# A four-layer macaron network on one Trainium2 core: expert rows, moments and norms by chunk, and another order in the mixers' fronts

## The chip, the cores and the metric

The kernel runs on one core of one Trainium2 chip. The metric is the device time in microseconds (us) of one execution; the time given for a kernel is the median of its runs. The engines are named as in the profile: PE is TensorE (PEld its weight loads), DVE is VectorE, ACT is ScalarE, POOL is GpSimd, SP is SyncE, which here issues most of the DMAs.

## The reference

The input is a stream x of 1024 tokens of 256 features, which goes through four layers. Each layer is a "macaron": half of a feed-forward network, a mixer, and half of a feed-forward network again, each behind a layer norm without weights:

```
def layernorm(x):  m, v = mean(x), var(x);  return (x - m) / sqrt(v + 1e-5)

for layer in 0..3:
    x = x + 0.5 * ffn[layer](layernorm(x))
    x = x +       attn[layer](layernorm(x))
    x = x + 0.5 * ffn[layer](layernorm(x))
```

What the eight blocks compute:

- `ffn[0]`: 32 experts, each token goes to its best 6, weighted by their softmax shares, plus a shared expert. `ffn[3]`: 8 experts, best 2, with a sigmoid router, plus a shared expert. Each expert is `(silu(x Wg) * (x Wu)) Wd`.
- `ffn[1]`: one 256 x 256 linear layer with binarized weights (sign times the mean absolute weight of the row) and a bias. `ffn[2]`: 8 experts of one linear layer, best 1.
- `attn[0]`: retention with 16 heads, a gate, a norm and a multi-layer perceptron. `attn[1]`: sparse attention. `attn[2]` and `attn[3]`: Mamba2 mixers with 8 and 64 heads. They project x, B, C, a gate z and a step dt; run a causal convolution of 4 taps and a silu over x, B and C; turn dt (softplus) and A into decays, with cumulative sums along the chunk; and combine chunk products with a running state.

## The kernel before

**Where the data is.** The stream x stays in SBUF from end to end, as `self.x` of 128 partitions x 8 chunks x 256 features; a chunk is 128 tokens, and 4 chunks (`CB`) are a half b (0 or 1). One method of a class `Net` is a stage; the twelve stages run one after the other in the order of the reference.

**Expert rows and how they reach x.** The expert stages `l0_ffn` and `l3_ffn` (both through `moe`) scatter their results, one row per token and choice (6 or 2 of them), into a table `rows` in HBM, and leave behind, in `self.pending[b]`, a function `add_rows(b)` (L640 to L654). Whoever needs half b of x next calls `settle(b)` (L153), which runs it. `add_rows` takes the half in two pairs of chunks: two DMAs of 768 KB for 6 rows (L644, on SyncE) into a buffer of the five-buffer weight pool, then for each chunk one VectorE add of three rows to three (L648, 128x768) and three adds into x (L651, 128x256). With 2 rows there are two adds. Four places settle: layer 0's mixer, layer 1's first FFN, layer 3's mixer, and the store at the end. The other norms have no rows to add.

**The norm.** `moments(b)` (L171) settles, then does `bn_stats` and `bn_aggr` for each of the 4 chunks on VectorE (L178, L179). `scales(b)` (L182) makes 1/sqrt(v + eps) for the four together on GpSimd, by an add (L187) and a pow (L188) of 128x4. `layernorm` (L191) norms each chunk on VectorE (L193). `transpose_tokens` (L165) turns the four chunks with TensorE (L168), and `evac` copies the PSUM bank of 128x512 to SBUF, by turns on VectorE (L126) and ACT (L128). `layernorm_T` (L202) ties these up as `measure`, `norm`, `turn`, and `row`, which is all three.

**Layer 0's mixer** (`l0_attn`, L707). It has its own `scales(b)` (L734 to L743), which needs two scales per token, hence two pows of 128x4 (L740, L742) per half. Ahead of its loop it runs `scales(0)`, `norm(0)`, `scales(1)`, then issues the loads of fc1 and fc2 on SyncE. The loop of 12 steps is a software pipeline over the chunks: in step s, scores of chunk s-2 (mask add L848), the norm of s+1 (L762 on VectorE, h0 L765 on ACT, two transposes L770), projections of s (L780, L783), rotation of s-1 (`turn`: L793 on GpSimd, L794 and L796 on VectorE), values and gate of s-2, output of s-3 (bias add on GpSimd at L928). Instructions go to each engine's in-order queue in the order of the source.

**Layer 1's FFN** (`l1_ffn`, L1030). For each half: `row(b)` for the whole half, one VectorE add of half the bias to the half (L1038, 128x1024), and for each chunk two matmuls into PSUM (L1042) and a VectorE add into x (L1045). `self.hb` and `self.bwT` (the bias and the transposed weights, both halved) are made ahead of time.

**The mixers of layers 2 and 3** (`mamba`, L1466). Ahead of a loop over steps stands a front, whose order is written out by hand under `in_order`, which keeps TensorE's, ACT's and VectorE's queues in source order (L1835 to L1905). Its pieces: `decay_sums(b)` is a generator in 8 parts, `d0` for half 0 and `d1` for half 1: dt's matmuls (L1518), softplus by Exp and Ln on ACT, dA (L1534), row sums (`ps_row`, L1544), their copy to `cr` and two DMAs into HBM (`rows`), sums `ps_cum` (L1562), and the decays `ps_dec` (L1567). `conv_b`, `conv_c` and `prep_front` each do a projection (L1577), a first tap on ACT (L1580), and give back the other three taps (VectorE, L1584) and a silu (ACT, L1588). `products` multiplies B and C, `prep_back` transposes x (L1659), `chunk` reads decay rows back from HBM, `exponents` (L1687) and `raised` (L1692, an Exp on ACT) turn them into weights. `few` is true for layer 2 (8 heads), where half 1's norm and decay parts lie in the front too; for layer 3 (64 heads) they are put in `later`, part by part, one per step of the loop.

## Time and profile before

| | us |
|---|---|
| runs | 2039.61, 2051.31, 2053.77; median 2051.31 |
| the profiled execution | 2134.34 |
| its span (first to last instruction) | 2132.1, mean granted TensorE clock 0.901 |
| busy in the span: PE, PEld, DVE | 1772.7 (83%), 1258.1 (59%), 1144.8 (54%) |
| busy in the span: ACT, POOL | 798.5 (37%), 879.1 (41%) |
| stretch from layer 0's first rows at 292.84 to its fourth mask add | 55.0 |
| first `l1_ffn`, first rows 744.98 to last add 784.51 | 39.5 |
| second `l1_ffn`, 905.34 to 924.70 | 19.4 |
| front of layer 2's mixer, 1014.0 to 1068.9 | 54.9 |
| front of layer 3's mixer, 1360.77 to 1420.02 | 59.3 |

How to read the profile: times are those of one profiled execution, which took longer than the timed runs. A group of instructions is a line of the code on one engine with its tiles; behind the bar stand its busy time, the mean of one in nanoseconds, and the time that the engine was idle just before them, with what ended that. The table by stretch gives for each engine the busy time and, in brackets, the number of instructions; then the clock that was granted to TensorE as a share of full speed, the busy share of the DMA engines, and GB/s. In the table of waits each line says which instruction waited for which, for how long in all, how many times, and the longest. The timeline gives start, length, engine, line, and in square brackets the idle time ahead. One TensorE matmul in 4-byte floats shows as two records.

### The profile page before, as it was taken

What the parts mean: (1) busy time and instruction counts of PE and PEld (TensorE: products, weight loads), DVE (VectorE), ACT (ScalarE), POOL (GpSimd) and SP (SyncE); (2) the same over time, 40 slices, a digit from 0 to 9 for tenths busy, and PEclk for the clock granted to TensorE, in tenths of its full rate; (3) what the DMA queues carried; (4) which work ended last, traced back from release to release, by engine and by line L of the source; (5) the groups of instructions that cost most, each with busy time, mean ns of one, the idle gap of its engine ahead of it and who ended that gap; (6) DMA issues with size and microseconds to landing.
All of it is one profiled execution on the core that took longest, in us unless ns stands there. A gap on an engine that the chain in (4) does not pass through costs nothing. (4 is left out here: it accounts for less than half of the span.)

```text
span 2132.1 us, 29472 instructions
## 1 busy us (share of the span) xinstructions
PE 1772.7 (83%) x10590; PEld 1258.1 (59%) x10590; DVE 1144.8 (54%) x2679; ACT 798.5 (37%) x1329; POOL 879.1 (41%) x821
## 2 busy tenths in 40 slices
PE   6898849898888737879687988569999999999885
PEld 4576626565666524554366456447777677777564
DVE  5432256316322268656564653377777767776533
ACT  1122214311122204510562012267877677777111
POOL 3466545330666430000042016124566537667253
PEclk8999969998999858979697989789999999999788
DMA  8255450040455340000221013243444444544132
GB/s 286 78 163 157 138 207 12 1 149 24 137 163 159 115 173 1 1 21 0 90 91 31 10 30 96 95 133 119 154 148 149 159 137 154 165 142 128 41 92 91
DMA packets 117438, 226.00 MB, mean 106 GB/s; under 512 B 22382, under 2 KB 68828, under 8 KB 117142
## 3 DMA queue, kind: packets, MB, share of 16 engines
q1 hardware_dynamic: 88134, 170.17, 24.6%
q0 software_dynamic: 20608, 48.45, 7.0%
q10 hardware_dynamic: 8528, 5.26, 0.8%
q8 instruction: 92, 1.51, 0.3%
q14 instruction: 76, 0.62, 0.1%
HBM read 195.13 MB, written 41.81 MB: 111 GB/s over the span
## 5 line engine op out<-in xcount | busy, mean ns | idle before, releaser
L475 POOL DMA_INDIRECT xe<-table,sl_get x176 | 179.8, 1022 | 228.5 <-DVE sl_get L451 146.7
L499 PE MATMUL ps_gu<-we,xeT 128*128 128x352 f32 x704 | 238.1, 481 | 0.0
L529 POOL DMA_INDIRECT rows<-ye,sl_put x176 | 177.0, 1005 | 139.7 <-ACT ye L128 45.6
L524 PE MATMUL ps_ye<-we,hT 88*128 88x256 f32 x704 | 178.6, 396 | 40.7 <-issue 14.1
L1584 DVE SCALAR_TENSOR_TENSOR xc<-pp,L_attn_cols,xc 128x511 f32<-128x511 f32 (+2 forms) x216 | 161.4, 747 | 48.5 <-ACT xc L1580 43.2
L524 PEld LDWEIGHTS ps_ye<-we,hT 88*128 88x128 f32 x704 | 134.7, 195 | 86.7 <-issue 19.6
L504 DVE SCALAR_TENSOR_TENSOR he<-se,xe,ps_gu 128x176 f32<-128x176 f32 x176 | 68.4, 396 | 208.4 <-issue 106.7
L499 PEld LDWEIGHTS ps_gu<-we,xeT 128*128 128x128 f32 x704 | 133.8, 202 | 59.3 <-issue 10.3
L187 POOL TENSOR_SCALAR ln_rstd<-ln_mv 128x4 f32<-128x4 f32 x22 | 5.1, 234 | 393.9 <-DVE ln_mv L179 389.4
L1711 PE MATMUL pz<-xT,wt 128*128 128x128 f32 x1152 | 145.1, 280 | 19.5 <-DVE state L1758 8.0
L1687 DVE SCALAR_TENSOR_TENSOR lm<-lm,jb,top 128x128 f32<-128x128 f32 x576 | 153.6, 340 | 0.0
L1711 PEld LDWEIGHTS pz<-xT,wt 128*128 128x128 f32 x1152 | 137.7, 195 | 25.2 <-issue 9.3
L1577 PE MATMUL pp<-xT,wx 128*128 128x512 f32 x288 | 145.2, 629 | 1.5 <-ACT dec L1568 0.9
L1784 PE MATMUL yacc<-wt,y 128*128 128x256 f32 x576 | 144.1, 393 | 0.7 <-POOL y L1766 0.7
L1766 POOL TENSOR_TENSOR y<-y,sg 128x512 f32<-128x512 f32 x72 | 91.7, 1274 | 108.4 <-DVE y L1765 107.1
L1704 POOL TENSOR_TENSOR ce<-ce,CT 128x1024 f32<-128x1024 f32 x54 | 128.0, 2370 | 0.0
L128 ACT COPY xT<-ps_tr 128x512 f32<-128x512 f32 x22 | 12.8, 584 | 293.4 <-PE ps_tr L168 264.9
L503 ACT ACTIVATE se<-ps_gu 128x176 f32<-128x176 f32 x176 | 54.7, 318 | 172.9 <-PE ps_gu L499 75.8
L1784 PEld LDWEIGHTS yacc<-wt,y 128*128 128x128 f32 x576 | 104.6, 191 | 24.1 <-issue 10.6
L1416 PE MATMUL ps_y<-w8T,xT 128*128 128x512 f32 x256 | 118.5, 617 | 0.0
L1739 PE MATMUL py<-lm,xt 128*64 128x128 f32 x1152 | 109.2, 284 | 6.2 <-issue 5.4
L168 PE MATMUL ps_tr<-cst,xn 128*128 128x128 f32 x176 | 41.9, 394 | 86.5 <-DVE xn L193 67.0
(383 smaller groups left out, 3552.4 us busy)
## 6 DMA issues: line engine op xcount, KB each, us to landing
lm<-rows SPq DMA_DIRECT2D x72, 512.0 KB
ce<-rows SPq DMA_DIRECT2D x54, 512.0 KB
rows<-zero POOLq DMA_DIRECT2D x16, 768.0 KB
y<-rows SPq DMA_DIRECT2D x16, 768.0 KB
we<-in_L_ffn_w_gate_dram SPq DMA_DIRECT2D x64, 176.0 KB
we<-in_L_ffn_w_up_dram SPq DMA_DIRECT2D x64, 176.0 KB
we<-in_L_ffn_w_down_dram SPq DMA_DIRECT2D x64, 176.0 KB
we<-in_L_ffn_w_dram SPq DMA_DIRECT2D x48, 176.0 KB
```

Of the source, the lines that this page charges most:

```text
L475: nc.gpsimd.indirect_dma_start(xe[:, i, :], None, table, bass.IndirectOffsetOnAxis(get[:, e * per + j : e * per + j + 1], 0), bounds_check ...
L499: nc.tensor.matmul(pg, xeT[:, k, i * P : (i + 1) * P], wgu[:, :, k], start=(k == 0), stop=(k == KD - 1))
L524: nc.tensor.matmul(py[:, i, :], hT[:, q, i * P : (i + 1) * P], wd[:, q, :], start=(q == 0), stop=(q == 1))
L529: put_rows = nc.gpsimd.indirect_dma_start(rows, bass.IndirectOffsetOnAxis(put[:, e * per + j : e * per + j + 1], 0), y[:, i, :], None, bou ...
L1416: nc.tensor.matmul(ps, xT[:, k, cs], self.w8T[:, k, 2 * e2 : 2 * e2 + 2, :], start=(k == 0), stop=(k == KD - 1))
L1577: nc.tensor.matmul(pp, wv[:, k, :], xT[:, k, b * S : (b + 1) * S], start=(k == 0), stop=(k == KD - 1))
L1584: nc.vector.scalar_tensor_tensor(out[:, 3 - w :], pp[:, : S - 3 + w], cw[:, m, w : w + 1], out[:, 3 - w :], ALU.mult, ALU.add)
L1687: nc.vector.scalar_tensor_tensor(k["lm"][:, h, :], k["lm"][:, h, :], jb[:, k["c"], n : n + 1], top, ALU.add, ALU.min)
L1704: nc.gpsimd.tensor_tensor(k["ce"], k["ce"], ct, ALU.mult)
L1711: nc.tensor.matmul(pz[:, m, :], u["wz"][:, kk, m * P : (m + 1) * P], xT[:, kk, c * P : (c + 1) * P], start=(kk == 0), stop=(kk == KD - 1),)
L1739: nc.tensor.matmul(py[i * HP : (i + 1) * HP, m, :], w[:, h * HP : (h + 1) * HP], v[:, h, :], start=(m == 0 and n == 0), stop=(n == len(src ...
L1784: nc.tensor.matmul(yacc[cc // 2][:, cc % 2, :], k["y"][:, m, :], u["wo"][:, m, :], start=(u["g"] == 0 and m == 0 and cc % 2 == 0), stop=(u ...
```

## The change

- `self.pending[b]` becomes a list of four functions, one per chunk; `settle(b, n, psum)` runs those of the first n chunks. The rows are still loaded in pairs of chunks by the same DMAs, all of a half at its first chunk.
- New helpers `moment`, `scale` and `centre` do the moments, the 1/sqrt (a pow of one column) and the norm of one chunk.
- Where `psum` is given, the six rows of a chunk are summed by six TensorE matmuls with the identity into a PSUM tile `ps_add`, and one VectorE add puts that into x.
- `l0_attn`: `scales` is by chunk, with one pow of two columns; chunks 0 and 1 go ahead of the loop, and chunk s+2 goes into step s, behind the scores and ahead of the norm of s+1. The loads of fc1 and fc2 are now issued ahead of the second half's rows.
- `l1_ffn` is written anew as a pipeline over 8 chunks in three parts: `front` (rows, moments, scale), `turn` (norm, two transposes, a copy on ACT, the bias add on GpSimd) and `back` (two matmuls, the add into x). Odd chunks' rows, where there are any, are summed on TensorE.
- `layernorm_T`'s `row` goes chunk by chunk (`by_chunks`) where rows are pending: that is half 0 of layer 3's mixer.
- The mixers' front: the projection of x's first block goes ahead of B's taps, the third and fourth decay parts of half 0 ahead of C's taps, and the taps of x's second block behind all eight parts; x's third silu goes ahead of `raised`; for layer 2 the first two parts of `d1` lie together ahead of `raised`; for layer 3 half 1's later parts begin with a free step.
- The store settles chunk by chunk.

The diff, without blank lines:

```diff
...
-    def settle(self, b):
-        if b in self.pending:
-            self.pending.pop(b)()
+    def settle(self, b, n=CB, psum=None):
+        parts = self.pending.get(b, [])
+        while len(parts) > CB - n:
+            parts.pop(0)(psum)
+        if not parts:
+            self.pending.pop(b, None)
...
+    def moment(self, pool, c):
+        st = pool.tile([P, 6], F32, name=f"ln_st{c}")
+        mv = pool.tile([P, 2], F32, name=f"ln_mv{c}")
+        self.nc.vector.bn_stats(st, self.x[:, c, :])
+        self.nc.vector.bn_aggr(mv, st)
+        return mv
+    def scale(self, pool, c):
+        nc = self.nc
+        mv = self.moment(pool, c)
+        rstd = pool.tile([P, 1], F32, name=f"ln_rs{c}")
+        nc.gpsimd.tensor_scalar(rstd, mv[:, 1:2], EPS, None, ALU.add)
+        nc.gpsimd.tensor_tensor(rstd, rstd, self.mhalf[:, 0:1], ALU.pow)
+        return mv, rstd
+    def centre(self, xn, c, mv, rstd):
+        self.nc.vector.tensor_scalar(xn, self.x[:, c, :], mv[:, 0:1], rstd, ALU.subtract, ALU.mult)
+        return xn
     def moments(self, pool, b):
...
         def row(b):
+            if b in self.pending:
+                by_chunks(b)
+                return
             measure(b)
...
+        def by_chunks(b):
+            xn = p.tile([P, CB, D], F32, tag="xn", name="xn")
+            ps = [psum.tile([P, S], F32, tag="mm", name="ps_tr") for _ in range(KD)]
+            ms = {}
+            for cc in range(CB + 1):
+                if cc < CB:
+                    self.settle(b, cc + 1)
+                    ms[cc] = self.scale(p, b * CB + cc)
+                if cc > 0:
+                    j = cc - 1
+                    self.centre(xn[:, j, :], b * CB + j, *ms[j])
+                    for k in range(KD):
+                        self.nc.tensor.transpose(
+                            ps[k][:, j * P : (j + 1) * P], xn[:, j, k * P : (k + 1) * P], self.ident
+                        )
+            for k in range(KD):
+                self.evac(xT[:, k, b * S : (b + 1) * S], ps[k])
         return xT, row, measure, norm, turn
...
-        def add_rows(b):
-            for c0 in range(b * CB, (b + 1) * CB, 2):
-                y2 = self.w("y2")[:, : 2 * K * D].rearrange("p (c n d) -> p c n d", c=2, n=K)
-                for i in range(2):
-                    nc.sync.dma_start(y2[:, i], rv[c0 + i, :, :K, :])
-                for i in range(2):
-                    y, xc, n = y2[:, i], self.x[:, c0 + i, :], K
-                    if n == 6:
-                        nc.vector.tensor_tensor(y[:, 0:3], y[:, 0:3], y[:, 3:6], ALU.add)
-                        n = 3
-                    for j in range(n):
-                        nc.vector.tensor_tensor(xc, xc, y[:, j], ALU.add)
+        ys = {}
+        def add_rows(b, cc, psum):
+            c, pair = b * CB + cc, cc // 2
+            if cc == 0:
+                for q in range(CB // 2):
+                    y2 = self.w("y2")[:, : 2 * K * D].rearrange("p (c n d) -> p c n d", c=2, n=K)
+                    for i in range(2):
+                        nc.sync.dma_start(y2[:, i], rv[b * CB + 2 * q + i, :, :K, :])
+                    ys[b, q] = y2
+            y, xc, n = ys[b, pair][:, cc % 2], self.x[:, c, :], K
+            if psum:
+                ps = psum.tile([P, D], F32, tag="mm", name="ps_add")
+                for j in range(n):
+                    nc.tensor.matmul(ps, self.ident, y[:, j], start=(j == 0), stop=(j == n - 1))
+                nc.vector.tensor_tensor(xc, xc, ps, ALU.add)
+                return
+            if n == 6:
+                nc.vector.tensor_tensor(y[:, 0:3], y[:, 0:3], y[:, 3:6], ALU.add)
+                n = 3
+            for j in range(n):
+                nc.vector.tensor_tensor(xc, xc, y[:, j], ALU.add)
         for b in range(B):
-            self.pending[b] = partial(add_rows, b)
+            self.pending[b] = [partial(add_rows, b, cc) for cc in range(CB)]
...
             h0 = sb.tile([P, NC, D], F32, name="h0")
-            rstd = sb.tile([P, NC], F32, name="ln_rstd")
-            rr = sb.tile([P, NC], F32, name="ln_rr")
+            sc = sb.tile([P, NC, 2], F32, name="ln_sc")
             nb = sb.tile([P, NC], F32, name="ln_nb")
...
-            def scales(b):
-                bs = slice(b * CB, (b + 1) * CB)
-                mv = mvs[b] = self.moments(sb, b)
-                var = mv[:, :, 1]
-                nc.gpsimd.tensor_scalar(rr[:, bs], var, 1.0 + EPS, EPS * EPS, ALU.mult, ALU.add)
-                nc.gpsimd.tensor_tensor(rr[:, bs], rr[:, bs], half[:, :CB], ALU.pow)
-                nc.gpsimd.tensor_scalar(rstd[:, bs], var, EPS, None, ALU.add)
-                nc.gpsimd.tensor_tensor(rstd[:, bs], rstd[:, bs], half[:, :CB], ALU.pow)
-                nc.vector.scalar_tensor_tensor(nb[:, bs], mv[:, :, 0], -1.0, rstd[:, bs], ALU.mult, ALU.mult)
+            def scales(c):
+                self.settle(c // CB, c % CB + 1)
+                mv = mvs[c] = self.moment(sb, c)
+                var = mv[:, 1:2]
+                nc.gpsimd.tensor_scalar(sc[:, c, 0:1], var, 1.0 + EPS, EPS * EPS, ALU.mult, ALU.add)
+                nc.gpsimd.tensor_scalar(sc[:, c, 1:2], var, EPS, None, ALU.add)
+                nc.gpsimd.tensor_tensor(sc[:, c, :], sc[:, c, :], half[:, :2], ALU.pow)
+                nc.vector.scalar_tensor_tensor(
+                    nb[:, c : c + 1], mv[:, 0:1], -1.0, sc[:, c, 1:2], ALU.mult, ALU.mult
+                )
...
                 nc.vector.tensor_scalar(
-                    hn, self.x[:, c, :], mvs[c // CB][:, c % CB, 0:1], rr[:, c : c + 1], ALU.subtract, ALU.mult
+                    hn, self.x[:, c, :], mvs[c][:, 0:1], sc[:, c, 0:1], ALU.subtract, ALU.mult
                 )
                 nc.scalar.activation(
-                    h0[:, c, :], self.x[:, c, :], AF.Identity, bias=nb[:, c : c + 1], scale=rstd[:, c : c + 1]
+                    h0[:, c, :], self.x[:, c, :], AF.Identity, bias=nb[:, c : c + 1], scale=sc[:, c, 1:2]
                 )
...
-            scales(0)
+            for c in range(2):
+                scales(c)
             norm(0)
-            scales(1)
             w2 = self.w("fc1")[:, : KD * F].rearrange("p (k f) -> p k f", k=KD)
...
                     scores(s - 2)
+                if s + 2 < NC:
+                    scales(s + 2)
                 if s + 1 < NC:
...
     def l1_ffn(self):
         nc, tc = self.nc, self.tc
-        with ExitStack() as es:
-            psM = es.enter_context(tc.tile_pool(name="f1m", bufs=8, space=PSUM))
-            xT, row, measure, norm, turn = self.layernorm_T(es, psM)
-            for b in range(B):
-                row(b)
-                xb = self.x[:, b * CB : (b + 1) * CB, :]
-                nc.vector.tensor_tensor(xb, xb, self.hb.unsqueeze(1).to_broadcast([P, CB, D]), ALU.add)
-                for c in range(b * CB, (b + 1) * CB):
-                    ps = psM.tile([P, D], F32, tag="mm", name="ps_y")
-                    for k in range(KD):
-                        nc.tensor.matmul(
-                            ps, xT[:, k, c * P : (c + 1) * P], self.bwT[:, k, :], start=(k == 0), stop=(k == KD - 1)
-                        )
-                    nc.vector.tensor_tensor(self.x[:, c, :], self.x[:, c, :], ps, ALU.add)
+        with tc.tile_pool(name="f1", bufs=3) as sb, tc.tile_pool(name="f1s", bufs=1) as st, tc.tile_pool(
+            name="f1m", bufs=8, space=PSUM
+        ) as psM:
+            ms, xts = {}, {}
+            def front(c):
+                self.settle(c // CB, c % CB + 1, psM if c % 2 else None)
+                ms[c] = self.scale(st, c)
+            def turn(c):
+                xn = self.centre(sb.tile([P, D], F32, tag="xn", name="xn"), c, *ms.pop(c))
+                pt = psM.tile([P, KD, P], F32, tag="mm", name="pt")
+                for k in range(KD):
+                    nc.tensor.transpose(pt[:, k, :], xn[:, k * P : (k + 1) * P], self.ident)
+                xts[c] = sb.tile([P, KD, P], F32, tag="xT", name="xT")
+                nc.scalar.copy(xts[c], pt)
+                nc.gpsimd.tensor_tensor(self.x[:, c, :], self.x[:, c, :], self.hb, ALU.add)
+            def back(c):
+                xT = xts.pop(c)
+                ps = psM.tile([P, D], F32, tag="mm", name="ps_y")
+                for k in range(KD):
+                    nc.tensor.matmul(ps, xT[:, k, :], self.bwT[:, k, :], start=(k == 0), stop=(k == KD - 1))
+                nc.vector.tensor_tensor(self.x[:, c, :], self.x[:, c, :], ps, ALU.add)
+            for c in range(NC + 2):
+                if c < NC:
+                    front(c)
+                if 0 <= c - 1 < NC:
+                    turn(c - 1)
+                if c >= 2:
+                    back(c - 2)
...
                 c_taps, c_silu = conv_c(0)
-                if few:
-                    measure(1)
-                b_taps()
                 next(d0)
...
                 if few:
+                    measure(1)
+                b_taps()
+                next(d0)
+                next(d0)
+                if few:
                     norm(1)
...
                 x[0][0]()
-                next(d0)
                 if few:
...
                     self.settle(1)
-                next(d0)
                 x.append(prep_front(us[0], 1))
-                x[1][0]()
                 next(d0)
...
                 next(d0, None)
+                x[1][0]()
                 for i in range(3):
...
                 prep_back(us[0], 0)
-                if few:
-                    next(d1)
                 exponents(ks[0])
                 x[2][0]()
+                x[2][1]()
                 prep_back(us[0], 1)
...
                 exponents(ks[1])
+                x[3][0]()
                 if few:
                     next(d1)
-                x[3][0]()
+                    next(d1)
                 raised(ks[0])
-                x[2][1]()
+                prep_back(us[0], 2)
                 if few:
...
                 x[3][1]()
-                prep_back(us[0], 2)
                 back = (us[0], NM - 1)
...
                 else:
-                    parts = [lambda: measure(1), lambda: norm(1), lambda: turn(1, 0), lambda: turn(1, 1)]
+                    parts = [lambda: measure(1), None, lambda: norm(1), lambda: turn(1, 0), lambda: turn(1, 1)]
                     parts += [d1.__next__] * 7 + [lambda: next(d1, None)]
-                    later = {i: [f] for i, f in enumerate(parts)}
+                    later = {i: [f] for i, f in enumerate(parts) if f}
...
         for b in range(B):
-            self.settle(b)
             for cc in range(CB):
+                self.settle(b, cc + 1)
                 self.nc.sync.dma_start(self.out[b, cc * P : (cc + 1) * P, :], self.x[:, b * CB + cc, :])
```

## The prediction

> **What bounds the kernel now.** I began with the page. The program spends most of its 2132.1 us span in expert and mixer loops that the change doesn't touch; the chain that ended last puts only small shares on the lines that it does touch. So the useful question is local: at each of the places where a norm follows expert rows, which engine waits, and for whom? Two groups of the page name it.
>
> ```profile
> L187 POOL TENSOR_SCALAR ln_rstd<-ln_mv 128x4 f32<-128x4 f32 x22 | 5.1, 234 | 393.9 <-DVE ln_mv L179 389.4
> L168 PE MATMUL ps_tr<-cst,xn 128*128 128x128 f32 x176 | 41.9, 394 | 86.5 <-DVE xn L193 67.0
> ```
>
> GpSimd's 393.9 us cost nothing by themselves (it has no other work then). TensorE's 67.0 us behind the normed rows are the candidate. I then cut the trace into the five stretches that change, each from its first ready operand to the instruction that starts the part which is the same in both kernels (columns: stretch, length, busy time and count by engine, granted clock, DMA share, GB/s).
>
> ```profile
> 292.84:347.80 54.96, 34.61 (x274) 22.01 (x275) 39.91 (x95) 17.74 (x45) 23.04 (x31) 0.76 0.44 162
> 744.98:784.51 39.53, 16.93 (x48) 12.59 (x48) 28.94 (x68) 1.17 (x2) 2.85 (x5) 0.56 0.68 244
> 905.34:924.70 19.36, 12.35 (x48) 9.92 (x48) 15.18 (x49) 1.17 (x2) 3.79 (x6) 0.74 0.16 56
> 1014.00:1068.90 54.90, 37.30 (x134) 23.44 (x132) 28.40 (x73) 32.45 (x49) 1.85 (x3) 0.69 0.25 87
> 1360.77:1420.02 59.25, 35.66 (x111) 20.83 (x111) 35.72 (x80) 28.75 (x42) 2.35 (x4) 0.72 0.47 156
> ```
>
> They are layer 0's mixer up to chunk 3's scores, layer 1's first and second FFN, and the fronts of the mixers of layers 2 and 3. Together 228.0 us, 11% of the span: that caps the change. Only in the first FFN is one engine (VectorE, 28.94 of 39.53) near its limit; its waits, and TensorE's, are
>
> ```profile
> DVE y L648 <- DMA y<-rows: 9.7, 1, 9.7
> DVE x L1045 <- PE ps_y L1042: 7.5, 7, 2.2
> DVE xn L193 <- POOL ln_rstd L188: 2.7, 2, 1.5
> ...
> PE ps_tr L168 <- DVE xn L193: 31.0, 2, 24.0
> ```
>
> The 9.7 us are rows still on their way, before my stretch begins; the change doesn't make them land earlier. The other 7.5 + 2.7 = 10.2 us, with the DVE work that can go elsewhere, are what can be won. TensorE works there in two bursts, and the clock says at what pace:
>
> ```profile
> 758.70 2.10 PE L168 MATMUL ps_tr<-cst,xn 128*128 128x128 f32 x8 [24.02 <-DVE xn L193]
> 761.64 6.00 PE L1042 MATMUL ps_y<-bwT,xT 128*128 128x256 f32 x16 [0.85 <-DVE xT L126]
> 774.58 2.19 PE L168 MATMUL ps_tr<-cst,xn 128*128 128x128 f32 x8 [6.94 <-DVE xn L193]
> 777.41 6.64 PE L1042 MATMUL ps_y<-bwT,xT 128*128 128x256 f32 x16 [0.64 <-DVE xT L126]
> ```
> ```profile
> 763.60:765.60 2.00, 2.00 (x6) 1.60 (x5) 0.56 (x2) 0.00 (x0) 0.00 (x0) 0.50 1.09 348
> 765.60:767.64 2.04, 2.04 (x8) 1.41 (x6) 1.71 (x5) 0.00 (x0) 0.00 (x0) 0.83 0.77 243
> 774.58:776.80 2.22, 2.19 (x8) 1.47 (x8) 2.19 (x5) 0.00 (x0) 0.00 (x0) 0.50 0.70 248
> ```
>
> Half clock for the first 7 us of work, full clock just as the burst ends, and half again after 6.94 us of idling.
>
> **The change, part by part.** *Layer 1's first FFN.* By duration, VectorE now does 8 row sums of 0.949 + 3 x 0.419 us = 2.21 (17.7), 8 x (0.412 + 0.174 + 0.407 + 0.421) of moments, norm and last add (11.3), two bias adds of 1.22 and two copies of 0.68 (3.8): 32.8, of which back-to-back overlap leaves 28.94 busy (0.88). The change turns four row sums into one add of 0.42 each and drops bias adds and copies: 4 x 2.21 + 4 x 0.42 + 11.3 = 21.8, about 19.3 busy, 4.8 per pair of chunks. TensorE gets, per pair, 6 matmuls of 128x256, which the records split in two: 12 x 0.375 = 4.5 at half clock (from 16 records in 6.00), 12 x 0.23 = 2.8 at full (16 in 3.72, the second burst of the second FFN); with 4 transposes and 8 records of ps_y a pair takes 4.5 + 1.1 + 3.0 = 8.6 cold, 2.8 + 0.5 + 1.9 = 5.2 warm. Being in order, TensorE also waits for ACT's copy (0.38) and GpSimd's pow, which could make a cold pair 9.7. GpSimd adds the bias: 8 adds of 128x256, 0.73 to 1.64 each (L928), and a pow of one column, estimated at 0.57 from 1.04 for 4 columns and 2.91 for 16; both lie beside VectorE unless the pow is late, for which I put 0.9 per chunk, so VectorE's warm pair is about 6.6. Two cold pairs (17.2), two warm (13.2), and the last chunk's tail 0.23 + 0.57 + 0.41 + 0.5 + 0.39 + 0.93 + 0.42 = 3.5: 33.9 to 34 instead of 39.5, **5.5 saved**. Bounds: all cold at 9.7 is 38.8 + 3 = 41.8, a loss of 2.3; all warm 26.4 + 3.5 = 29.9, a gain of 9.6.
>
> [...] The row says about 7 us with a gap of 0.85 in it; a pipeline with gaps in each chunk I put at 14 to 17. I take the row.
>
> [...] Moments and norms were already one instruction per chunk; what becomes smaller is the bias add (1.22 for 4 chunks; 8 x 0.42 would have been 3.4 instead of 2.4), and it goes to GpSimd. [...]
>
> *The second FFN* has no rows. Per chunk: bn 0.4, aggr 0.17, norm 0.41, add 0.42 on VectorE, 1.4 in all; GpSimd 0.23 + 0.57 + 0.73 to 1.64, hence 1.5 to 2.4; TensorE 2.0 cold, 1.2 warm. The fill ahead of the first transpose falls from 4 chunks of moments to one (4.5 us of TensorE idling in the trace), but 8 chunks at 1.6 to 2.0 and a tail of 3 are 16 to 19. I take 16.8, **2.5 saved** (2.9 lost to 5 gained). If GpSimd's adds take 1.64 it sets the pace: 8 x 2.4 + 3 = 22.2, 2.9 lost.
>
> *Layer 0's mixer.* First project now starts at 311.0, behind 4 chunks of rows and four 128x4 pows (1.04 each). After: 2 chunks of rows (2 x 2.8 with moments), one pow of two columns (0.72) per chunk, hn, transposes, hT: about 304.5. But the sums of chunks 2 to 7 (2.8 each) now stand inside the first six steps, in VectorE's queue ahead of the norm and the rotation (L794, L796), for which TensorE's scores wait. Before, chunks 4 to 7 ran in the gap ahead of the first rotation. The first scores mask (L848) comes 6.8 earlier (328.5 to 321.7), the second 3.2 (that step holds 12.6 us of VectorE's work against a period of 10), the third 2.6. **3.5 saved**, 0 to 8. Rows of the second half (SyncE) are now issued behind fc1 and fc2, and their buffers come free with chunks 1 and 3; they are needed some 15 us later, the same loads ahead of the first FFN ran at over 300 GB/s, and fc1 itself is needed only after step 8, so I price it at 0; without that cover a 768 KB load late costs about 2.5.
>
> *Layer 3's front.* Two rows per chunk, moments and transposes by chunk: xT some 2 us earlier (copies end at 1372.6 before). Then the decay chain goes first (dt, dA, row sums) and its HBM rows leave at about 1388 instead of 1392.9, but nothing waits for those rows then. VectorE waits about 1.8 for ACT's Ln in the chain, and the projection of x's second block stands behind the first's taps (1390 instead of 1389.1). B's silu stays near 1396.1. Later x3's silu is earlier in ACT's queue by one place but behind two exponents. **0.5 saved** (3 lost to 5 gained). The second half's moments, norm, turn move one step later in a loop of 32 steps: hidden, 0.
>
> *Layer 2's front* has the same order and two steps of the second decay chain ahead of `raised` on ACT, each with exponent tables (1.28 a load): raised 1057.8 to about 1059.4. Queued behind it on ACT is x3's silu, 0.5 later, and for that TensorE's transposes wait: **0.5 lost** (3 lost to 3 gained).
>
> *The store* has each chunk's rows added and stored as before: 0. Fewer GpSimd columns elsewhere: 0.
>
> Sum: 5.5 + 2.5 + 3.5 + 0.5 - 0.5 = 11.5. The profiled execution took 2134.3 us, 2.2 outside its span, at a mean granted clock of 0.90, and is 83 us (4%) above the median of the runs, 2051.3; scaled by 0.96 the gain is 11. I predict 2051.3 - 11.3 = **2040.0**.
>
> **Rivals.** *Fuller overlap.* VectorE idles 15.0 in layer 0's stretch, 10.6 and 4.2 in the FFNs, and TensorE 17.6 and 23.6 in the fronts. If half of it goes in layer 0 and the second FFN (7.5, 2.1), [...] and a quarter in the fronts (4.4, 5.9): 28, 2023. For it: in each stretch no engine is above 80%. Against: chains inside a step stay as they were. *The row sums at half clock.* If gaps keep TensorE cold in the first FFN, it sets the pace: 5.5 become -2.3, 2048. For it: clock 0.56 there. *The fronts lose the clock (slower).* If the decay chain, put first, leaves TensorE idle before x's blocks for long enough to fall to 0.50 for the rest of the front, layer 2's 37.3 busy us at 0.69 become 51.5 and layer 3's 35.7 at 0.72 become 51.4: 14 + 16 = 30 lost at most, and from 11.5 on it outweighs the rest. At two thirds: 2051 - 11 + 20 = 2060. Against it: both fronts have projections (0.63 to 0.78 each) to fill in. *The change does nothing of note*: if layer 0's steps are set by what they hold, its 3.5 come back, 2043.5; this lies inside my range.
>
> **How the numbers follow.** Likeliest case 0.58 (2040, own range 2033 to 2048, the zero-effect variant within it); fuller overlap 0.26 (2016 to 2033); half clock 0.09 (2044 to 2053); fronts slower 0.07 (2052 to 2080). The range 2019 to 2054 leaves out about 0.05 at the fast end and 0.05 at the slow one, and a little for the runs' own spread (2039.6 to 2053.8). About 1% (20.5 us; below 2030.8, above 2071.8) is what a measurement of this kernel can tell: faster 0.26 (nearly all of fuller overlap, a little of the likeliest), slower 0.04, within 0.70.
>
> **What would show it.** First FFN: granted clock near 0.5 for the first 15 us and 1.0 later, ps_add at 4.5 then 2.8 per chunk, stage 34 us. Layer 0: first project at about 11.7 after the rows land instead of 18.2, but third mask only 2.6 earlier. Second FFN about 17. Fronts within 3 of before. Wrong if GpSimd's bias adds take over 1.6 us and hold the last add, if layer 0's gain stays at 7 or more to its end, or if the fronts' clock changes by over 0.1.

## The result, and the profile after

The changed kernel takes 2035.32 us (median of 20 runs, 2026.4 to 2042.55); the kernel before, in as many runs beside it, 2048.22 (2039.39 to 2055.21). The ratio is 0.9941, 95% interval 0.9927 to 0.9956: 12 us less, between 9 and 15. 2040 was forecast from a median of 2051.3, 11.3 less.

The two profiled executions differ by far more than that (2132.1 and 2036.9 us of span). 79 of these 95 us lie in the four stretches that end with the landing of expert rows, in which the expert stages run, and these the change does not edit: 292.84 against 255.88, 268.5 against 242.2, 124.7 against 120.4, 131.4 against 119.7. They are left out, and the other stretches are compared one by one, each from its own start.

| stretch | before | after | forecast |
|---|---|---|---|
| layer 0's mixer, first rows to last add into x | 183.63 | 184.97 | 3.5 less |
| layer 1's first FFN, first rows to last add | 39.54 | 34.82 | 5.5 less |
| layer 1's mixer | 120.91 | 118.60 | |
| layer 1's second FFN, to its last add | 19.26 | 18.55 | 2.5 less |
| layer 2's first FFN | 88.87 | 87.04 | |
| layer 2's mixer | 140.10 | 140.51 | 0.5 more |
| layer 3's mixer, first rows to first `py` | 59.25 | 56.66 | 0.5 less |
| layer 3's mixer, first rows to last add | 626.25 | 617.96 | |

Of the page's two groups that the prediction began with, only the first is still listed: five of its 22 instances, the adds of eps ahead of a pow, have become adds of one column elsewhere.

```profile
L213 POOL TENSOR_SCALAR ln_rstd<-ln_mv 128x4 f32<-128x4 f32 x17 | 3.9, 231 | 230.2 <-DVE ln_mv L205 225.6
```

The table by stretch of the changed kernel, for the same five stretches (the first one of the same length as before):

```profile
255.88:310.84 54.96, 35.98 (x244) 22.40 (x248) 39.77 (x98) 17.02 (x42) 27.19 (x47) 0.81 0.45 162
...
683.03:717.85 34.82, 24.22 (x96) 19.18 (x96) 22.95 (x52) 2.98 (x8) 14.77 (x25) 0.85 0.78 277
...
836.45:855.00 18.55, 11.75 (x48) 8.65 (x48) 13.91 (x44) 2.98 (x8) 13.21 (x26) 0.79 0.18 58
942.19:997.70 55.51, 36.74 (x134) 22.91 (x134) 31.25 (x76) 31.28 (x48) 3.84 (x4) 0.69 0.23 87
1286.31:1342.97 56.66, 35.93 (x111) 21.41 (x111) 37.80 (x81) 28.71 (x42) 5.72 (x10) 0.69 0.50 164
```

Read the second line first: in the first FFN VectorE's work fell from 28.94 to 22.95 us, TensorE's rose from 16.93 to 24.22, and TensorE's granted clock rose from 0.56 to 0.85. In the first line VectorE's work is the same as before (39.77, 39.91), while GpSimd's rose from 23.04 to 27.19. In the fronts of layers 2 and 3, the last two lines, little moved.

The waits in the first FFN, of VectorE and of TensorE:

```profile
DVE y L707 <- DMA y<-rows: 10.0, 1, 10.0
DVE xn L194 <- POOL ln_rs L190: 4.0, 5, 1.3
DVE x L1118 <- PE ps_y L1117: 3.7, 4, 1.4
DVE x L704 <- PE ps_add L703: 3.0, 2, 2.2
```
```profile
PE ps_add L703 <- DMA y<-rows: 13.2, 1, 13.2
PE pt L1108 <- DVE xn L194: 7.6, 4, 2.7
```

TensorE's 31.0 us behind the normed rows have become 7.6. VectorE's 7.5 + 2.7 have become 3.7 + 4.0 + 3.0, so its waits are no shorter between these two kernels; experiment 10 takes the gain apart. The sums of the rows themselves, from TensorE's timeline of the changed kernel:

```profile
685.54 5.22 PE L703 MATMUL ps_add<-y,cst 128*128 128x256 f32 x12 [13.17 <-DMA y<-rows]
690.59 0.38 PE L1108 MATMUL pt<-cst,xn 128*128 128x128 f32 x2
693.70 0.65 PE L1108 MATMUL pt<-cst,xn 128*128 128x128 f32 x2 [2.73 <-DVE xn L194]
...
695.85 3.43 PE L703 MATMUL ps_add<-y,cst 128*128 128x256 f32 x12
699.11 0.38 PE L1108 MATMUL pt<-cst,xn 128*128 128x128 f32 x2
...
709.80 2.75 PE L703 MATMUL ps_add<-y,cst 128*128 128x256 f32 x12
```

The table by stretch, cut where the granted clock changes, goes with it:

```profile
685.54:690.38 4.84, 4.84 (x12) 3.85 (x13) 3.61 (x8) 0.00 (x0) 2.30 (x3) 0.50 1.00 409
690.38:693.79 3.41, 0.69 (x5) 0.38 (x4) 1.96 (x7) 0.37 (x1) 1.63 (x5) 1.00 1.02 425
693.79:697.20 3.41, 3.41 (x10) 2.75 (x11) 2.65 (x5) 0.37 (x1) 2.16 (x2) 0.50 1.02 393
697.20:717.85 20.65, 15.28 (x74) 12.17 (x72) 12.35 (x31) 2.23 (x6) 8.68 (x16) 1.00 0.64 197
```

Full clock comes twice. It comes first 4.84 us after the first matmul, at the end of the first odd chunk's sums (5.22), and two transposes take 0.38 there. TensorE then idles for 2.73 us, for VectorE's norm, so that it has only 0.69 us of work in 3.41 us of full clock, and is back at half (two transposes take 0.65). At 697.20, in the middle of the next sums (3.43), full clock comes again and stays: from there six rows take 2.75.

### The profile page after: what moved, and what is told of

The parts are those of the page before. It is cut to its first block, busy times and chain, and to the rows that moved or that the text cites. A ratio compares the mean times of both kernels' runs of the same rounds, so it can differ in the third digit from the quotient of the medians.

```text
span 2036.9 us, 29663 instructions
## 1 busy us (share of the span) xinstructions
PE 1756.2 (86%) x10638; PEld 1258.1 (62%) x10638; DVE 1138.3 (56%) x2665; ACT 799.0 (39%) x1336; POOL 907.4 (45%) x883
## 5 line engine op out<-in xcount | busy, mean ns | idle before, releaser
L547 PE MATMUL ps_gu<-we,xeT 128*128 128x352 f32 x704 | 232.5, 472 | 0.0
L572 PE MATMUL ps_ye<-we,hT 88*128 88x256 f32 x704 | 168.3, 380 | 2.9 <-ACT ye L128 1.7
L1858 POOL TENSOR_TENSOR sqs<-sqs,sq 128x512 f32<-128x512 f32 x56 | 71.3, 1273 | 94.5 <-ACT sq L1857 94.5
L1777 DVE TENSOR_TENSOR lm<-lm,M 128x1024 f32<-128x1024 f32 x72 | 87.1, 1215 | 42.6 <-ACT lm L1773 41.1
```

The lines of the kernel that those rows point to most:

```text
L547: nc.tensor.matmul(pg, xeT[:, k, i * P : (i + 1) * P], wgu[:, :, k], start=(k == 0), stop=(k == KD - 1))
L572: nc.tensor.matmul(py[:, i, :], hT[:, q, i * P : (i + 1) * P], wd[:, q, :], start=(q == 0), stop=(q == 1))
```

## The experiments

Each of the twelve kernels ran in five rounds beside the kernel before; ratios are to that, and a difference in us of the whole program is worked out from the ratio, so it is not quite that of the medians. Differences of stretches are from the profiles, one for each kernel. For four kernels (7., 8., 9. and 12.) the kernel before itself took 2128 to 2132 us, and their profiles have the surplus again in the expert stretches; a ratio compares runs of the same rounds.

**1. Layer 1's FFN alone.** The kernel before, with the helpers, with add_rows and the store by chunk, and with this:

```diff
-            for b in range(B):
-                row(b)
...
+            for c in range(NC + 2):
+                if c < NC:
+                    front(c)
+                if 0 <= c - 1 < NC:
+                    turn(c - 1)
+                if c >= 2:
+                    back(c - 2)
```

> The kernel before with only layer 1's FFN in its new form (layer 0's mixer, the fronts of both mixers and layer 3's norm as before). Theory by stages: the first FFN takes 34.8 us instead of 39.5, the sparse attention behind it 2 less because it starts on a warmer TensorE, the second FFN and the stage behind it 2 to 2.5 less: 8.5 to 9.5 us below the kernel before, about two thirds of the whole gain of 12.9. Rival: the mixers' fronts carry the gain, and what layer 1 wins is returned by the stages behind it: 3 to 4 us below before.

Measured: 2039.49 against 2047.70, ratio 0.9966 (0.9953 to 0.9980): 7.0 less, 4 to 10. The first FFN took 34.27, the second 18.55. So layer 1 brings over half of the gain, nearer to the first theory (8.5 to 9.5) than to the rival (3 to 4), though the interval shuts out neither. But the mixer behind it took 122.77, more than before (120.91), with the same granted clock in its first 20 us (0.66), and layer 2's mixer, whose code is that of before, 136.39 instead of 140.10. The stages behind are not passive; more on that below.

**2. Layer 0's mixer as before, in the changed kernel.**

```diff
-            for c in range(2):
-                scales(c)
+            scales(0)
             norm(0)
+            scales(1)
...
-                if s + 2 < NC:
-                    scales(s + 2)
```

> The changed kernel with layer 0's mixer as it was before. Theory: by chunk, layer 0's mixer loses 1.3 us (184.97 against 183.63 from its first rows to its last add), so this kernel has 183.6 there and is 1 to 2 us faster than the changed one, 14 to 15 below before. Rival (the prediction's own step): the chunks' form gains 3.5 there and the trace of before was short by chance: this kernel is 3 to 4 slower than the changed one, 9 to 10 below before.

Measured: 2035.14 against 2047.70, ratio 0.9943 (0.9922 to 0.9964), not to be told from the changed kernel. The stretch took 183.21, as the theory had it. Over all kernels of this study, the six with the changed form of this mixer took 184.97, 186.49, 185.01, 185.94, 186.16 and 186.07 (mean 185.8), the five with the old form 183.63, 185.23, 183.21, 182.64 and 183.08 (mean 183.6). The change loses 2.2 us here: the rival, a gain of 3.5, falls.

**3. and 4. Why layer 0 lost.** In the changed kernel the waits of VectorE up to the third mask add begin so, behind the landing:

```profile
DVE ln_nb L800 <- POOL ln_sc L799: 8.7, 7, 1.4
DVE t L855 <- POOL t L852: 3.6, 3, 1.6
```

Seven times VectorE waits for the chunk's pow, only to make the small product `ln_nb`. The first edit moves that product one step on:

```diff
             def scales(c):
...
-                nc.vector.scalar_tensor_tensor(
-                    nb[:, c : c + 1], mv[:, 0:1], -1.0, sc[:, c, 1:2], ALU.mult, ALU.mult
-                )
...
             def norm(c):
...
+                nc.vector.scalar_tensor_tensor(
+                    nb[:, c : c + 1], mvs[c][:, 0:1], -1.0, sc[:, c, 1:2], ALU.mult, ALU.mult
+                )
```

> The changed kernel, with only the small product ln_nb of a chunk moved from its scales (step s) to its norm (step s+1). Theory: VectorE's 7 waits for GpSimd's pow at ln_nb (8.7 us in 57) are what turned layer 0's gain into a loss; without them the third mask add comes 3 to 5 us earlier against the first rows (52 to 54 instead of 57.0) and the stage takes 180 to 182, 15 to 17 below before. Rival: VectorE's row sums, put into the steps, set the pace, and the wait only moves to the next operand: stage 184 to 185, no change.

Measured: 2035.04 against 2047.70, ratio 0.9936 (0.9913 to 0.9959). Third mask add 55.35 behind the first rows (56.97 in the changed kernel's profile, 58.0 in the mean of the six with its form), stretch 183.33, which is 2.5 under the mean of the six: between theory and rival. Part of the wait went to another operand of the same pow: 3.7 us at `hn`, and 2.6 still at `ln_nb`. What stayed is on ACT and TensorE. ACT's timeline and TensorE's, of the changed kernel:

```profile
305.57 0.60 ACT L824 ACTIVATE h<-x,ln_nb,ln_sc 128x256 f32<-128x256 f32 x1 [5.99 <-DVE ln_nb L800]
306.08 0.56 ACT L938 COPY oT<-po 128x512 f32<-128x512 f32 x1
306.54 0.37 ACT L974 COPY odT<-pt_d 128x256 f32<-128x256 f32 x1
306.81 0.60 ACT L877 COPY kT<-pt_kT 128x512 f32<-128x512 f32 x1
307.28 0.61 ACT L877 COPY qT<-pt_qT 128x512 f32<-128x512 f32 x1
```
```profile
306.97 1.16 PE L882 MATMUL pkv<-va,t 128*128 128x128 f32 x8 [3.80 <-ACT odT L974]
```

ACT has stood idle for 5.99 us ahead of one h0 (6.57 in experiment 3's kernel), which nobody needs before that chunk's output, four steps further on, and four copies that TensorE needs now stand behind it in order. So the second edit takes `ln_nb` and h0 out of `norm` into a function `late`, calls it at the end of the step and fixes ACT's order there:

```diff
+                with self.in_order(tail, ("Activation",)):
...
                     if 0 <= s - 2 < NC:
                         gate(s - 2)
+                    if s < NC:
+                        late(s)
```

> The changed kernel with a chunk's ln_nb and its h0 (the second norm, on ACT) put at the end of the step, behind the copies of odT, kT and qT in ACT's queue, and ACT's order there fixed. Theory: in the changed kernel ACT idles 6.6 us ahead of one h0, which waits for GpSimd's pow by way of ln_nb, and the copies that TensorE waits for (3.8 us) stand behind it; without that the third mask add comes at 52 to 54 against the first rows instead of 57, and the stage takes 180 to 182. Rival: GpSimd, with the gate's pow (2.9), the rotation (1.65) and now a pow per chunk, sets the pace of the step: third mask 55 to 57, stage 183 to 185.

Measured: 2034.72 against 2047.84, ratio 0.9937 (0.9912 to 0.9962). Third mask add at 52.34, stretch 182.00, both as the theory had them. pkv no longer waits for odT; TensorE's next wait is 3.56 us, for a normed chunk that stands behind the pow. Against the changed kernel's profile that is 3 us less in the stretch, against the mean of its form 3.8, against the old form 1.6. The edit also fixes ACT's order, and what that alone does was not tried. In the time of the whole program it can't be told.

**5. The mixers' fronts and the free step as before.**

```diff
+                x[1][0]()
                 next(d0)
                 next(d0)
                 next(d0, None)
-                x[1][0]()
...
-                    next(d1)
                     next(d1)
                 raised(ks[0])
...
-                    parts = [lambda: measure(1), None, lambda: norm(1), lambda: turn(1, 0), lambda: turn(1, 1)]
+                    parts = [lambda: measure(1), lambda: norm(1), lambda: turn(1, 0), lambda: turn(1, 1)]
```

> The changed kernel with the hand-written order of both mixers' fronts, and the parts left for the loop, as before. Theory by stages: layer 3's mixer goes back from 618 to 621 to 626, layer 2's stays within 0.5: 5 to 10 us below before. Rival: the 8 us of layer 3's mixer lie between two executions and not between two programs, since its loop is the same: this kernel stays 12 below before, and its layer 3 mixer takes 618 to 621.

Measured: 2040.89 against 2047.70, ratio 0.9967 (0.9955 to 0.9978): 6.8 less, so fronts and free step together are worth about 5 of the 12 (1 to 9). Layer 3's mixer took 624.05: the theory held, the rival fell. Layer 2's took 136.42, 4 less than with the new order, which the theory did not have.

**6. and 7. The free step.** First the changed kernel without it:

```diff
-                    parts = [lambda: measure(1), None, lambda: norm(1), lambda: turn(1, 0), lambda: turn(1, 1)]
+                    parts = [lambda: measure(1), lambda: norm(1), lambda: turn(1, 0), lambda: turn(1, 1)]
```

> The changed kernel with half 1's parts of layer 3's mixer back in loop steps 0, 1, 2, ... (no free step behind the moments). Theory: in step 1 VectorE's four norms of half 1 then stand beside three GpSimd instructions (y times sg, xd, ce) and take about 5.1 us instead of 2.3, the state add behind them is late, and TensorE's z waits some 4 us for it; steps 1 to 9 give back 4 to 10 us, and layer 3's mixer takes 620 to 627 instead of 618. Rival: the new order of the front brings the gain, and the free step is hidden in a loop of 32 steps, as the prediction had it: within 1 us of the changed kernel in steps 1 to 9.

Measured: 2043.75 against 2047.84, ratio 0.9986 (0.9972 to 0.9999): only 2.9 below before. Some nine of the twelve us (5 to 13) hang on this one word. Layer 3's mixer took 622.00, as the theory had it. Next to experiment 5, which lacks the new order of the fronts too and is 6.8 below before, the new order comes out as a loss of about 4 (0 to 8), as much as layer 2's mixer shows (140.49 here, 136.42 there); layer 3's first y is as early in both (58.78 and 59.07 behind the first rows). Then the kernel before with the free step and nothing else:

```diff
-                    parts = [lambda: measure(1), lambda: norm(1), lambda: turn(1, 0), lambda: turn(1, 1)]
+                    parts = [lambda: measure(1), None, lambda: norm(1), lambda: turn(1, 0), lambda: turn(1, 1)]
```

> The kernel before with one edit alone: the free step behind half 1's moments in layer 3's mixer loop. Theory: half 1's four norms take 2.3 us instead of 5.1 there, steps 1 to 9 of the loop win 8 to 11 us against the first step, and the total falls by 6 to 10, about as much as all of layer 1 brings. Rival: the free step helps only together with the new order of the front, because that frees VectorE or the rows earlier: steps 1 to 9 win less than 3, total within 2 of before.

Measured: 2123.05 against 2131.59, ratio 0.9950 (0.9929 to 0.9971), 10.7 less: the theory held. The start of each step's y (us behind the first rows) shows where:

| step | before | free step alone | won | changed | changed, no free step |
|---|---|---|---|---|---|
| 0 | 60.73 | 60.46 | 0.3 | 57.86 | 58.78 |
| 1 | 69.80 | 69.53 | 0.3 | 66.94 | 67.86 |
| 2 | 82.59 | 78.17 | 4.4 | 75.58 | 79.78 |
| 5 | 110.50 | 103.63 | 6.9 | 101.62 | 108.00 |
| 7 | 133.53 | 122.58 | 10.9 | 120.57 | 131.01 |
| 9 | 152.06 | 140.85 | 11.2 | 138.84 | 150.77 |

At step 16, when half 1's parts are done in both kernels, 11.4 us of the time since step 0 are still won: it is not work put off.

Step 2 first. Half 1's four norms on VectorE, in the kernel before, what GpSimd did meanwhile, and TensorE's z behind them:

```profile
1431.16 5.09 DVE L193 TENSOR_SCALAR xn<-x,ln_mv,ln_rstd 128x256 f32<-128x256 f32 x4
1436.18 0.68 DVE L1758 TENSOR_TENSOR state<-state,pst 128x512 f32<-128x512 f32 x1
```
```profile
1431.39 1.30 POOL L1766 TENSOR_TENSOR y<-y,sg 128x512 f32<-128x512 f32 x1 [1.29 <-DVE y L1765]
1432.66 1.09 POOL L1727 TENSOR_TENSOR xd<-xt,dec 128x512 f32<-128x512 f32 x1
1433.71 2.40 POOL L1704 TENSOR_TENSOR ce<-ce,CT 128x1024 f32<-128x1024 f32 x1
```
```profile
1436.91 3.78 PE L1711 MATMUL pz<-xT,wt 128*128 128x128 f32 x16 [3.97 <-DVE state L1758]
```

Four norms take 1.38 us where GpSimd rests (layer 1's first FFN). Here they take 5.09, and GpSimd works for 4.79 of it. The first takes 0.41; the other three, one by one:

```profile
1431.49 1.36 DVE L193 TENSOR_SCALAR xn<-x,ln_mv,ln_rstd 128x256 f32<-128x256 f32 x1
1432.77 1.13 DVE L193 TENSOR_SCALAR xn<-x,ln_mv,ln_rstd 128x256 f32<-128x256 f32 x1
1433.82 2.44 DVE L193 TENSOR_SCALAR xn<-x,ln_mv,ln_rstd 128x256 f32<-128x256 f32 x1
```

Each starts 0.1 us behind one of GpSimd's instructions and ends some 0.15 behind it. GpSimd's are hardly longer than without the norms (1.27, 1.05 and 2.37 in the changed kernel, from 1354.07 on). The state add after them is late, and z waits 3.97. With the free step the norms stand beside y times sg alone:

```profile
1362.50 2.33 DVE L219 TENSOR_SCALAR xn<-x,ln_mv,ln_rstd 128x256 f32<-128x256 f32 x4
```

(the changed kernel; beside it GpSimd's y times sg, 1.30 from 1362.73: one norm takes 1.36, the other three 0.40 or 0.41). In both traces a norm that begins just behind a GpSimd instruction lasts about as long as that one: 1.36, 1.13 and 2.44 beside 1.30, 1.09 and 2.40 before, 1.36 beside 1.30 in the changed kernel. What makes it last so long is not shown here.

Behind the wait TensorE is slow as well: in the next 6.09 us it was granted 0.57 of its clock. From the output product (`yacc`) in step 1 to that in step 2 15.79 us pass before, and 9.93 with the free step alone.

Steps 5 to 9 are another matter. The same count puts what is won there at one place: from the output product in step 6 to that in step 7 15.34 us pass before, and 8.62 with the free step alone. In the five kernels whose decay parts lie where they were before it is 15.1 to 15.3, in the nine others 8.62. Between the other steps up to 12 the two kernels differ by at most 1.7 us, either way. VectorE's timeline at the end of step 6 in the kernel before, and TensorE's z of step 7:

```profile
1482.30 0.42 DVE L1531 SCALAR_TENSOR_TENSOR dt<-dt,dt 128x256 f32<-128x256 f32 x1
...
1485.69 0.28 DVE L1537 TENSOR_SCALAR dt<-dt 128x256 f32<-128x256 f32 x1
1485.89 2.15 DVE L1687 SCALAR_TENSOR_TENSOR lm<-lm,jb,top 128x128 f32<-128x128 f32 x8
1487.96 0.68 DVE L1758 TENSOR_TENSOR state<-state,pst 128x512 f32<-128x512 f32 x1
```
```profile
1488.69 2.68 PE L1711 MATMUL pz<-xT,wt 128*128 128x128 f32 x16 [3.98 <-DVE state L1758]
```

Five VectorE instructions of a decay part (L1531 to L1537, 3.7 us) stand ahead of eight exponents and the state add, and z waits 3.98 for that add. Then TensorE ran 4.61 us at 0.63 of its clock; z took 2.68 instead of 1.95. With the free step the five fall into step 7:

```profile
1482.61 0.42 DVE L1531 SCALAR_TENSOR_TENSOR dt<-dt,dt 128x256 f32<-128x256 f32 x1
...
1485.27 0.29 DVE L1537 TENSOR_SCALAR dt<-dt 128x256 f32<-128x256 f32 x1
1485.82 1.22 DVE L1696 TENSOR_TENSOR lm<-lm,M 128x1024 f32<-128x1024 f32 x1 [0.27 <-ACT lm L1692]
```
```profile
1485.87 1.95 PE L1711 MATMUL pz<-xT,wt 128*128 128x128 f32 x16
```

Step 7 is the last of its four chunks: by the source such a step has no exponents at its end and no state add, and the z behind it, of step 8, shows no wait.

A rival is on ACT. `raised` has its Exp in every other step; before, the decay part's Exp (L1526) lay in a step between, and cost a table load of its own and a way back to silu's. One step later it lies right behind `raised` and needs none; the same goes for the Exp of `cr`. From step 0's y to step 10's, ACT loads a table 17 times in the kernel before and 13 times with the free step, at 1.28 us each. But these loads held nothing up: around the first two that fall away (1464.96 and 1469.37) TensorE was busy for the whole of 1463.80 to 1484.71, at full clock and at 8.62 to 8.63 us a step, and around the other two (1506.36 and 1510.92) for 32.91 of 34.00 us, at full clock again.

**8. and 9. Are these two gains separate?** The first attempt moved only the norm, in the changed kernel:

```diff
-  None, lambda: norm(1), lambda: turn(1, 0), lambda: turn(1, 1)]
+  None, lambda: both((lambda: norm(1), lambda: turn(1, 0))), lambda: turn(1, 1)]
```

> The changed kernel with only half 1's norm moved one step in layer 3's loop (norm and first turn together in step 2, second turn in step 3, decay parts from step 4 on as before). Theory: the norm's wait at step 1 costs about 4 of the 10 us; the other 4 to 6 come from the decay parts, which fall on other steps (odd and even steps of the loop hold different work), so steps 1 to 2 win 4 against the kernel with no free step and the gains at steps 5 and 7 are gone: total 3 to 6 above the changed kernel. Rival: the norm is all of it, and the total is within 1 of the changed kernel.

Measured: 2137.13 against 2131.59, ratio 1.0027 (1.0011 to 1.0044), slower than before, and by the ratios 18 us above the changed kernel, more than either theory had. Step 2 kept its gain (76.67), the gains at steps 5 and 7 were gone (108.93, 131.72). But step 3 came at 91.01 instead of 85.38: the first turn now stands in the same step as the norm, and TensorE waits up to 2.4 us for the normed chunks, so the edit added a stall of its own. It is no clean test. Its layer 3 mixer took 625.61, 7.6 more than the changed kernel's; where the rest of the 18 us lies is not known. The second put the free step behind the norm, in the kernel before:

```diff
-                    parts = [lambda: measure(1), lambda: norm(1), lambda: turn(1, 0), lambda: turn(1, 1)]
+                    parts = [lambda: measure(1), lambda: norm(1), None, lambda: turn(1, 0), lambda: turn(1, 1)]
```

> The kernel before with the free step behind half 1's norm instead of ahead of it: the norm stays in step 1 beside GpSimd's three instructions, while the turns and the decay parts move one step. Theory: the two halves of the free step's gain are separate. The norm still takes 5.1 us and z waits for the state, so nothing is won at step 2 (against the first step, within 1 of before); the decay parts' Exp falls into the steps that hold the Exp of raised, ACT loads its table four times less by step 10 (1.28 each), and steps 5 to 9 win 6 to 7: total 5 to 7 below before. Rival: the norm's delay is the root and what was won at steps 5 and 7 followed from it: less than 2 won by step 9, total within 2 of before.

Measured: 2122.22 against 2128.15, ratio 0.9965 (0.9947 to 0.9983), 7.5 less. Norm and z are as before:

```profile
1433.34 5.10 DVE L193 TENSOR_SCALAR xn<-x,ln_mv,ln_rstd 128x256 f32<-128x256 f32 x4
1439.09 3.43 PE L1711 MATMUL pz<-xT,wt 128*128 128x128 f32 x16 [4.46 <-DVE state L1758]
```

Against step 1, 0.9 was won at step 2 and 7.8 by step 9. From the output product in step 1 to that in step 2 it is 14.94 us, as slow as before, and from step 6 to step 7 it is 8.62. The two gains are separate, as the theory had it: of the 11.4 us won at step 16, 6.9 are won here, so about 4.5 are the norm's and 7 the decay part's. The theory put the latter to ACT's table loads, of which there are 13 here too; TensorE's timeline puts it to the state add of step 6.

**10. The rows on VectorE.** The changed kernel without TensorE's sums:

```diff
-                self.settle(c // CB, c % CB + 1, psM if c % 2 else None)
+                self.settle(c // CB, c % CB + 1, None)
```

> The changed kernel with all expert rows of layer 1's first FFN summed on VectorE (the pipeline by chunk stays). Theory: VectorE has 4 x (2.2 - 0.4) = 7 us more work of 0.88 busy each, so the stage takes 39 to 41 us, no better than the 39.5 before: the gain of 5 comes from TensorE's sums. Rival: the pipeline alone carries the gain, because the cold TensorE's 5.2 us of sums in the first pair set the pace: 34 to 36.

Measured: 2041.97 against 2047.84, ratio 0.9976 (0.9965 to 0.9987). The stretch took 37.22, between the two theories: 2.3 less than before by the pipeline, another 2.4 by the sums.

```profile
684.33:721.55 37.22, 17.35 (x48) 11.30 (x48) 28.41 (x64) 2.98 (x8) 14.62 (x25) 0.53 0.69 245
```

VectorE's 28.41 is as much as before (28.94), and its idle time fell from 10.6 to 8.8: that is the pipeline. The sums take 5.5 us more off its work and give 3.1 back as waiting. TensorE stays at 0.53 of its clock. The whole program loses 7 us against the changed kernel, and only 2.4 of them here. In the profile the mixer behind it (120.59), layer 2's first FFN (88.92) and its mixer (141.99), all of the same code as in the changed kernel, are 5.4 longer together, but layer 3's mixer (610.94), also unchanged, is 7.0 shorter; where the rest lies is not shown.

**11. Layer 3's norm for the whole half.**

```diff
-            if b in self.pending:
-                by_chunks(b)
-                return
```

> The changed kernel with layer 3's first norm for the whole half again. Theory: the transposed x comes 1 to 2 us later and all of the front with it: first py 59 to 60 us behind the first rows instead of 57.9, the total 1 to 2 above the changed kernel. Rival: VectorE's taps set the front, and the norm's form is hidden: 57.9 as before, no change.

Measured: 2035.63 against 2047.84, ratio 0.9938 (0.9914 to 0.9962). The first y came at 61.45 behind the first rows, against a mean of 58.9 of the seven kernels with by_chunks and the new front (57.86 to 59.89): a little more than the theory had. In the total it is not to be seen. The two kernels with by_chunks and the old front have it at 59.07 and 58.84: it is by_chunks that makes layer 3's first y earlier, not the new order.

**12. What the runs point to.** Layer 1, by_chunks and the free step as changed, layer 0 as in the second edit of experiments 3 and 4, both fronts in the old order: the diffs of experiments 4 and 5 on the changed kernel, but for one line of the latter, which stays

```diff
                     parts = [lambda: measure(1), None, lambda: norm(1), lambda: turn(1, 0), lambda: turn(1, 1)]
```

> What the runs so far point to, in one kernel: layer 1 and layer 3's norm as changed, the free step, layer 0 by chunk with h0 behind the copies, and the old order of both mixers' fronts. Theory: against the changed kernel layer 0's mixer is 2.5 to 3.5 us shorter, layer 2's mixer 2, layer 3's front even: 3 to 5 below the changed kernel, 15.5 to 18 below before. Rival: what a stage wins is lost again in the stages behind it, which meet another clock: within 2 of the changed kernel.

Measured: 2118.21 against 2131.59, ratio 0.9933 (0.9909 to 0.9956), against 0.9941 (0.9927 to 0.9956) of the changed kernel. Layer 0's stretch took 182.38 and layer 2's mixer 136.40, both as planned, but layer 1's mixer took 122.74 instead of 118.60. It beats the kernel before; that it beats the changed kernel is not shown.

## Why the prediction was right, and where only its sum was

2040.0 was forecast and 2035.3 measured, inside the range, with the change within 1% as the likeliest case had it. By its steps, though, that is in good part luck: layer 0 was put 5.7 us too low, and a gain of 10.9 that it had at nothing made up for it.

| step | forecast | measured |
|---|---|---|
| first FFN | -5.5 | -4.7 (-4.4 by the means of 10 and 3 kernels) |
| second FFN | -2.5 | -0.7 at the last add, -2.4 at TensorE's last product |
| layer 0's mixer | -3.5 | +2.2 (means of 6 and 5 kernels) |
| layer 3's front, to its first y | -0.5 | -1.1 (58.9 against 60.0, means of 7 and 4 kernels) |
| layer 2's front | +0.5 | +1.7 at equal clock |
| half 1's parts one step later | 0 | -10.9 by step 9 |

The terms measured add up to some -13 (the second FFN's taken at its last add), against a total of -12, between -15 and -9. The forecast's own sum of 11.5 scaled by 0.96 is 11.0; it took off 11.3.

*First FFN: right, by another course of the clock.* "Two cold pairs (17.2), two warm (13.2)" and a tail of 3.5 were forecast. From the first rows to the first add of ps_add it was 7.8 us, then 8.4, 6.8 and 6.5 between those adds (16.3 and 13.3), and 5.3 for the tail. The forecast put full clock at 14 to 17 us, the author's estimate from the first burst of before. It came after 4.84, was granted for 3.41 in which TensorE idled for 2.73, went back to 0.50 for another 3.41, and came to stay after 11.7. So full clock first came far earlier than the forecast had it, and what the sum left out is the gap of 2.73 behind it and the 3.41 us at 0.50 that followed. The pipeline and the sums bring about half of the gain each (2.3 and 2.4).

*Second FFN: the step that failed is the last add.* TensorE's last product was done 2.4 us earlier, 15.64 us into the stage, as the forecast of 16.8 wanted it. But VectorE's last add began 2.5 us after that. It stands behind the next stage's moments and norms, and these wait for a pow of four columns:

```profile
853.93 0.73 DVE L219 TENSOR_SCALAR xn<-x,ln_mv,ln_rstd 128x256 f32<-128x256 f32 x2 [0.85 <-POOL ln_rstd L214]
854.58 0.41 DVE L1118 TENSOR_TENSOR x<-x,ps_y 128x256 f32<-128x256 f32 x1
```

So outside `in_order` an engine's queue does not keep the order of the source, where that add comes first. The next stage's first FFN is 1.8 shorter (87.04 against 88.87), but that is not shown to be this gain: of the eleven kernels with the new second FFN five have 87.0 to 87.1 there and six 88.6 to 88.9, the three with the old one 88.6 to 88.9.

*Layer 0: the step that failed is "one pow of two columns (0.72) per chunk, hn, transposes, hT: about 304.5", carried on to the third mask add.* Its beginning was exact: the first project 11.79 us behind the rows (11.7 forecast), the first mask add 6.6 earlier (6.8). The third mask add was forecast 2.6 earlier and came 1.0 later (2.1 by the means of the six and five kernels). The sum counted VectorE's work per step. It did not ask which queues the chunk's pow enters: GpSimd's, behind the gate's pow (2.9) and the rotation (1.65), then VectorE's through `ln_nb`, then ACT's through h0, with TensorE's copies behind it. The kernel with h0 behind the copies takes out that chain: third mask 3.7 earlier than before, stretch 1.6 less, which is half of the forecast's gain. The reading that only the first FFN has an engine near its limit was off too: by its own table VectorE was as busy in layer 0's stretch (39.91 of 54.96).

*Layer 2's front: the right delay, passed on in full.* "raised 1057.8 to about 1059.4" was forecast, 1.6. With full clock granted at the entry to both (1.00 in the first 10 us), `raised` came 40.50 us into the mixer in the old order and 42.13 in the new, 1.63 later. But the first `py` came 1.67 later too (51.63 and 53.30), not 0.5, and the mixer's end 1.9 later. At 0.66 of the clock at the entry `py` came at 55.34 in the old order and 56.96 in the new (experiment 10), 1.6 later again.

*Layer 3: the step that failed is "move one step later in a loop of 32 steps: hidden, 0".* It was the largest term of all, and it lies outside the five stretches whose 228.0 us were to cap the change. What hides a moved part is not the length of the loop (64 steps, 32 for each half) but what else is in the step. Two places in the trace of before would have priced it: the four norms at 5.09 beside GpSimd with the 3.97 wait of z behind them, and the decay part's five VectorE instructions ahead of the state add with the 3.98 wait of z behind that.

The rivals: row sums at half clock did not come (0.85), nor did fronts that lose the clock (0.69 in both); fuller overlap in layer 0 was held off by the pow (that rival's 28 holds 8 for the first FFN, the author's estimate, which no trace showed). That the gain in layer 0 is given back in the steps was named as a variant, and came.

## What to carry to other kernels

A part that is moved into another step of a full loop has a price by what shares that step: put down, for each engine, which instructions it will stand beside and which it will stand ahead of, and look for the small result at the end of the step (here the state add) for which another engine waits. Here waits of TensorE of 3.97 and 3.98 us cost 6 to 7, with 0.57 and 0.63 of the clock granted behind them. Ahead of any small product that joins two engines, such as a bias of one column, ask what stands behind its reader in an in-order queue; here a late `ln_nb` held ACT for 5.99 us ahead of one h0 of 0.60, and TensorE waited 3.80 us for a copy behind it. And when a forecast's total is right, its terms still have to be measured one by one.
